# A macaron block of MoE, attention and MoE on one core: an eviction moved to ScalarE and GpSimd, attention's weights loaded among the experts, attention's tiles begun three slots later

## The chip, the core and the metric

The kernel runs on one core of a Trainium2 chip. The core has TensorE (PE: matmuls, with weight loads shown as PEld), VectorE (DVE), ScalarE (ACT), GpSimd (POOL) and SyncE (SP, which here only issues DMAs). Each engine works through its own queue in order and waits on semaphores for the others. The metric is the device time of one execution in microseconds, as a median over runs. A profile is one further execution, recorded instruction by instruction.

## The reference

4096 tokens of 256 channels (2 x 2048) go through three residual steps, with 16 attention heads in groups of 64 tokens, and 8 experts of which each token takes 2:

```python
def ffn(x):                                   # router_w, rg, ru, rd: experts; sg, su, sd: shared
    xn = x * rsqrt(mean(x * x) + eps)
    p, i = top_k(softmax(xn @ router_w.T), 2)
    rw = p / sum(p)
    # each expert takes its first 640 tokens, in token order
    routed = scatter_add(w * ((silu(xg @ rg) * (xg @ ru)) @ rd))      # 256 -> 1024 -> 256
    return (silu(x @ sg) * (x @ su)) @ sd + routed                    # 256 -> 2048 -> 256

def attn(x):
    q, k, v = split(x @ w_qkv)
    q, k = rmsnorm(q) * ln_w, rmsnorm(k) * ln_w
    return (softmax(causal(q @ k.T / 4)) @ v) @ w_proj                # inside groups of 64 tokens

x = x + 0.5 * ffn(layernorm(x))
x = x + attn(layernorm(x))
x = x + 0.5 * ffn(layernorm(x))
```

## The kernel before

Every float32 operand of a matmul is split into a high and a low float16 part, and each product is three matmuls (high x high, high x low, low x high: TERMS, line 35). `split` (line 101) makes such a pair of a weight: ACT scales and casts the high part, DVE subtracts to get the low part.

The shared FFN works on 8 blocks of 512 tokens. `shared` (line 379) runs 16 chunks of 128 hidden columns. In each, `gate_up` (line 326) does 12 matmuls into two PSUM tiles `pgu` (three buffers), ACT applies Silu (or Tanh, with an extra DVE step at line 344), DVE multiplies (line 349), ACT casts to `hh` (line 351) and DVE subtracts to `hl` (line 352). The 12 `down` matmuls of a chunk (line 360) are deferred until after the next chunk's `gate_up`; they add up in two PSUM tiles `outs` of 256 tokens each. After the last chunk, `fin` evicts both: DVE scales a tile and adds the residual `xr` (line 393), and SP stores it (line 396). `late` is the chunk at which the residual is loaded: 2, except for the last block in stage d, where it is 10. The eviction of a block thus stands, in program order, behind the first chunk of the next block.

The routed experts (`experts`, line 422) run one after the other, each with 8 chunks. A chunk loads three float32 pieces by SP (`re`, `re2`, two buffers), splits them on ACT and DVE, and runs 24 + 15 matmuls. After an expert's last chunk its five output tiles `eo` are scaled by the token weights (three on DVE, line 458, two on ACT, line 456), and POOL scatters each with an adding indirect DMA (line 459). There are four `eo` buffers. The five scatters of an expert are declared independent of each other; the first of the next expert waits for them. `expert_load` (line 403) fetches the next expert's tokens and tags.

Attention works on 32 tiles of 128 tokens. `attn_tile` (line 506) is a generator of some 27 steps: load, statistics, normalised `z` (ACT, line 159), transposes by SP, q/k/v (PE), the split into QK (ACT, POOL), scores, softmax (POOL lines 583 and 594, ACT lines 591 and 593), V copies (ACT, line 587), the weighted sum, projection, and statistics and split of the result for the second FFN. The fourth tile of each block then runs `route`, whose last steps are 8 indirect scatters on POOL for that block (line 317).

Four stages follow each other:

- a: the first FFN's front (statistics, routing) for 32 tiles, interleaved with shared blocks 0 to 3.
- b: the 8 experts of the first FFN.
- c: `attn_init` loads and splits attention's weights; then the shared blocks 4 to 7 of the first FFN and blocks 0 to 6 of the second run, 11 blocks and 176 chunks, with the attention tiles interleaved.
- d: the 8 experts of the second FFN, and its shared block 7.

The interleaving is written out: `drive` (line 720) takes one step of the block at a time, and after every three (`RATE_C`, one chunk) makes a slot of `Tiles.steps` (line 685), in which each living tile does one step. A new tile starts at every fourth slot (`GAP_C`), when `slot == nxt * gap`. At the end of a block, the whole last slot is emitted at once. That fixes the program order; the order on each engine is then made by the framework, which schedules by a simulated timeline (line 857) and may bring work forward whose inputs and buffers are free. SP's queue carries all loads, stores and transposes; POOL's carries the indirect DMAs beside its arithmetic.

Lines the change touches: `fin` in `shared` (388 to 398), `experts` (422, 453, 462, 467), `attn_init` (471 to 486), and the start of stage c in `macaron` (806 to 812).

Of the kernel before, what the change touches and what calls it, by code (L numbers as in the profile page):

```python
# [8 lines left out]
F32 = mybir.dt.float32  # L9
F32R = mybir.dt.float32r  # L10
F16 = mybir.dt.float16
# [4 lines left out]
ALU = mybir.AluOpType  # L16
# [4 lines left out]
P = 128  # L21
H = 256
# [3 lines left out]
WS = 16.0  # L26
XP = UP * WS
NB = 8
BT = 512
# [8 lines left out]
class Net:  # L38
# [340 lines left out]
    def shared(self, b, xb, src, dst, tanh=False, late=2):  # L379
        nc = self.nc  # L380
        outs = [self.ps_out.tile([P, BT], F32, name="po", tag="po") for _ in range(2)]
        for c in range(16):
            if c == late:
                res = self.res_load(src, b)
            h = [a[:, 0:BT] for a in self.hbuf()]
            yield from self.gate_up(self.sgu[:, c], xb, h, tanh)

            def fin(c=c, h=h):
                self.down(outs, 4, h, self.sdw[:, :, c], c, 16)
                if c < 15:  # L390
                    return
                for i in range(2):
                    nc.vector.scalar_tensor_tensor(
                        out=res[i], in0=outs[i].rearrange("p (t f) -> p t f", f=H), scalar=0.5 / WS,
                        in1=res[i], op0=ALU.mult, op1=ALU.add)
# [23 lines left out]
            out=w, in0=tag[:, :, 3], scalar=float(e), in1=tag[:, :, 1], op0=ALU.is_equal, op1=ALU.mult)  # L419
        nc.vector.tensor_tensor(out=w, in0=w, in1=tag[:, :, 2], op=ALU.add)  # L420

    def experts(self, R, rg, ru, rd, cur):

        nc = self.nc
        for e in range(E):
            x, ids, wts = cur["x"], cur["id"], cur["w"]
            outs = [self.ps_out.tile([P, BT], F32, name="po", tag="po") for _ in range(3)]
            cur = {}
            nxt = self.expert_load(R, e + 1, cur) if e < E - 1 else iter(())
            for c in range(8):  # L430
                r = self.raw.tile([P, 2, 2, P], F32, name="re", tag="raw")
                for i, s in enumerate((rg, ru)):
                    nc.sync.dma_start(
                        out=r[:, i], in_=s[e, :, c * P:(c + 1) * P].rearrange("(k p) f -> p k f", p=P))
                r2 = self.raw.tile([P, H], F32, name="re2", tag="raw2")
                nc.sync.dma_start(out=r2, in_=rd[e, c * P:(c + 1) * P])
                wc = self.raw.tile([P, 2, 2, 2, P], F16, name="wc")
                self.split(wc[:, 0], wc[:, 1], r)
                wd = self.raw.tile([P, 2, H], F16, name="wd")
                self.split(wd[:, 0], wd[:, 1], r2)  # L440
                h = self.hbuf()
                for t0, n in SUBS:
                    hs = [a[:, t0:t0 + n] for a in h]
                    for _ in self.gate_up(wc, x[:, :, t0:t0 + n], hs):
                        pass

                def fin(e=e, c=c, h=h, wd=wd, outs=outs, ids=ids, wts=wts):
                    self.down(outs, 5, h, wd, c, 8)
                    if c < 7:
                        return  # L450
                    key = R["key"], e
                    for t in range(5):
                        eo = self.raw.tile([P, H], F32, name="eo", bufs=4)
                        o = outs[t // 2][:, (t % 2) * H:(t % 2 + 1) * H]
                        if t % 2:
                            nc.scalar.activation(eo, o, AF.Copy, scale=wts[:, t:t + 1])
                        else:
                            nc.vector.tensor_scalar_mul(eo, o, wts[:, t:t + 1])  # L458
                        i = nc.gpsimd.indirect_dma_start(  # L459
                            out=R["acc"][:, :], out_offset=bass.IndirectOffsetOnAxis(ap=ids[:, t:t + 1], axis=0),  # L460
                            in_=eo, in_offset=None, bounds_check=T - 1, oob_is_err=False, compute_op=ALU.add).ins
                        if t:
                            self.tc.declare_no_dep(i, group=str(key), reason="an expert's tokens are distinct")
                        self.tc.add_to_no_dep_group(str(key), i)

                self.defer(fin)
                next(nxt, None)
            for _ in nxt:
                pass

    def attn_init(self, w_qkv, ln_w, w_proj):
        nc = self.nc
        a = self.at
        self.wqkv = a.tile([P, 2, 2, 3 * H], F16, name="wqkv")
        self.wpr = a.tile([P, 2, 2, H], F16, name="wpr")
        for k in range(2):
            for c0, n in ((0, 2 * H), (2 * H, H)):
                r = a.tile([P, 2 * H], F32, name="rq", tag="q32")[:, :n]
                nc.sync.dma_start(out=r, in_=w_qkv[k * P:(k + 1) * P, c0:c0 + n])
                self.split(self.wqkv[:, 0, k, c0:c0 + n], self.wqkv[:, 1, k, c0:c0 + n], r)  # L480
        wp = w_proj.rearrange("(j r c) f -> r j c f", r=2, c=16)
        for k in range(2):
            r = a.tile([P, H], F32, name="rp", tag="yy")
            for j in range(8):
                nc.sync.dma_start(out=r[j * 16:(j + 1) * 16], in_=wp[k, j])
            self.split(self.wpr[:, 0, k], self.wpr[:, 1, k], r)
# [227 lines left out]
def run_slots(tiles, until):  # L714
    while not until():
        for _ in tiles.steps():
            pass
# [22 lines left out]
def macaron(ctx, tc, x, w_qkv, ln_w, w_proj, router_w, rg, ru, rd, sg, su, sd, out):  # L740
    nc = tc.nc
    x = x.rearrange("b s h -> (b s) h")
    out = out.rearrange("b s h -> (b s) h")
    n = Net(ctx, tc)
    R1 = n.route_init(0)
# [5 lines left out]
    first = {}, {}  # L751
# [36 lines left out]
    def all_shared(key, b, src, dst, **k):  # L788
        yield from n.shared(b, fbs[key]["xb"], src, dst, **k)
        used.add(key)  # L790

    with n.phase("a", BT, 2, 16):
# [5 lines left out]
        tiles = Tiles(tile1, 32, GAP_A)  # L798
# [5 lines left out]
            drive(fed(main, weights) if b == 0 else main, tiles, RATE_A)  # L804
        run_slots(tiles, tiles.done)
    with n.phase("b", CAP, 3):
        n.experts(R1, rg, ru, rd, first[0])
    with n.phase("c", BT, 2, 6, SLC):
        n.attn_init(w_qkv, ln_w, w_proj)
        tiles = Tiles(tile2, 32, GAP_C)  # L810
        for b in range(NA, NB):
            drive(all_shared((1, b), b, R1["acc"], R1["acc"], tanh=True), tiles, RATE_C)
        for b in range(NC):
            run_slots(tiles, ready(2, b))
            drive(all_shared((2, b), b, x2, R2["acc"], tanh=True), tiles, RATE_C)
        run_slots(tiles, tiles.done)
# [16 lines left out]
SLC = 2  # L833
# [28 lines left out]
```

## Time and profile before

| what | us |
|---|---|
| median of 3 runs | 1830.85 (1830.73 to 1833.56) |
| the profiled execution's own time | 1834.82 |
| its span, first to last instruction | 1833.1 |
| PE busy in it | 1779.5 (97%) |
| DVE, ACT, POOL busy | 1199.9, 952.9, 751.3 |
| mean granted TensorE clock | 0.998 of full speed |

In time order, stage b is full from about 295 to 605, stage c begins at 605 and its last evictions are at 1453, and stage d takes the rest.

A timeline row reads: start, duration, engine, line, operation, output<-inputs, shape, count; in square brackets, how long the engine had stood idle before it and what ended that. A group row has its count after the x, then busy time and the mean in nanoseconds, then the idle time before the group with what ended it. A stretch row gives the stretch, its length, and the busy time of PE, PEld, DVE, ACT and POOL (instructions after the x), the granted clock, the share of DMA engines busy and GB/s. Idle time of an engine costs something only where PE waits for it in the end.

### The profile page before, as it was taken

Reading aid. Unit: us, or ns where it says so; the run is one execution under the profiler, and the core shown is the slowest. Engines: PE = TensorE matmul, PEld = TensorE weight load, DVE = VectorE, ACT = ScalarE, POOL = GpSimd, SP = SyncE. Lnnn points to the kernel's source line nnn. Section 1 sums busy time; section 2 is a strip of 40 time slices with the busy share of each in tenths; the row PEclk is TensorE's granted clock in tenths of the full one; section 3 lists DMA queues with packets and bytes.
Section 4 is the critical chain, followed back from the end, with each engine's and each line's share of the span. In section 5 each row is a group of like instructions: output and inputs, shape, how many; then the busy total and the mean of one; then the engine's idle time right before and its main releaser. Section 6 shows DMA issues by size and latency. Waiting matters only on the chain.

```text
span 1833.1 us, 37526 instructions
## 1 busy us (share of the span) xinstructions
PE 1779.5 (97%) x13724; PEld 1197.0 (65%) x13724; DVE 1199.9 (65%) x2891; ACT 952.9 (52%) x2055; POOL 751.3 (41%) x1072
## 2 busy tenths in 40 slices
PE   7899999999999899999999999999999999999998
PEld 4555556777777556666666666665655677777765
DVE  7754445666666567878777878787656566666643
ACT  5433234555555366666666666666323455555542
POOL 6755530112211334567767676776430011112210
PEclk9999999999999999999999999999999999999999
DMA  7532042455543346668576776766213044455420
GB/s 219 146 90 77 3 88 54 107 118 124 118 113 90 73 77 112 122 118 146 113 146 124 133 142 117 144 101 126 52 27 80 28 111 111 107 120 122 102 47 12
DMA packets 439194, 185.96 MB, mean 101 GB/s; under 512 B 302305, under 2 KB 436125, under 8 KB 439008
## 3 DMA queue, kind: packets, MB, share of 16 engines
q1 hardware_dynamic: 420528, 161.60, 40.7%
q0 software_dynamic: 17664, 21.17, 6.5%
q8 instruction: 107, 1.75, 0.4%
q10 hardware_dynamic: 816, 0.79, 0.1%
q14 instruction: 79, 0.65, 0.1%
HBM read 78.95 MB, written 42.21 MB: 66 GB/s over the span
## 4 chain that ended last, share of the span: by engine, by line
PE 36%; issue 32%; POOL 12%; DVE 10%; DMA 5%; ACT 4%; SPq 0%; POOLq 0%; another core or an unknown queue 0%; DVEq 0%; ACTq 0%
PE pgu L336 22%; PE po L360 11%; POOL xg L317 3%; DVE sl L349 2%; DMA acc<-eo,eidscatter 2%; DVE sl L344 1%; DVE hl L352 1%; POOL X L315 1%; POOL rstd L149 1%; POOL acc L459 1%; ACT hh L351 1%; PE pqk L636 1%; POOL S L583 1%; DVE st L144 1%; POOL e L594 1%
## 5 line engine op out<-in xcount | busy, mean ns | idle before, releaser
L336 PE MATMUL pgu<-xb,sgu 128*128 128x512 f16 x3072 | 742.4, 380 | 18.1 <-DVE sl L349 7.7
L351 ACT CAST hh<-sl 128x512 f16<-128x512 f32 (+2 forms) x512 | 272.8, 533 | 482.9 <-DVE sl L349 466.6
L336 PE MATMUL pgu<-xe,wc 128*128 128x384 f16 (+1 forms) x3072 | 497.0, 299 | 0.0
L336 PEld LDWEIGHTS <-sgu 128*128 128x128 f16 x3072 | 293.4, 98 | 292.9 <-issue 25.8
L349 DVE SCALAR_TENSOR_TENSOR sl<-pgu,sl 128x512 f32<-128x512 f32 (+2 forms) x512 | 300.2, 587 | 227.3 <-PE pgu L336 193.4
L352 DVE TENSOR_TENSOR hl<-sl,hh 128x512 f16<-128x512 f32 (+2 forms) x512 | 311.2, 608 | 161.5 <-ACT hh L351 155.1
L360 PEld LDWEIGHTS <-hh 128*128 128x128 f16 x3328 | 320.3, 98 | 112.3 <-ACT hh L351 7.9
L336 PEld LDWEIGHTS <-wc 128*128 128x128 f16 x3072 | 300.5, 98 | 92.0
L360 PE MATMUL po<-sdw,hh 128*128 128x256 f16 x2048 | 350.1, 273 | 8.1 <-issue 2.8
L360 PE MATMUL po<-sdw,hl 128*128 128x256 f16 x1024 | 247.1, 273 | 14.3 <-DVE hl L352 13.4
L360 PE MATMUL po<-wd,hh 128*128 128x256 f16 x1280 | 223.6, 273 | 0.0
L459 POOL DMA_INDIRECT out_dram<-eo,eidscatter x40 | 65.1, 1627 | 342.1 <-DVE eo L458 332.3
L360 PEld LDWEIGHTS <-hl 128*128 128x128 f16 x1664 | 162.8, 98 | 58.6 <-DVE hl L352 24.2
L347 ACT ACTIVATE sl<-pgu 128x384 f32<-128x384 f32 (+1 forms) x336 | 158.9, 473 | 71.1 <-PE pgu L336 35.5
L459 POOL DMA_INDIRECT acc<-eo,eidscatter x40 | 65.7, 1643 | 296.5 <-DVE eo L458 286.8
L317 POOL DMA_INDIRECT xg<-X,di x128 | 132.3, 1034 | 70.4 <-issue 27.5
L360 PE MATMUL po<-wd,hl 128*128 128x256 f16 x640 | 152.5, 273 | 1.1 <-DVE hl L352 1.1
L344 DVE SCALAR_TENSOR_TENSOR sl<-sl,pgu 128x512 f32<-128x512 f32 x176 | 119.9, 681 | 48.1 <-ACT sl L343 46.1
L343 ACT ACTIVATE sl<-pgu 128x512 f32<-128x512 f32 x176 | 104.2, 593 | 45.3 <-PE pgu L336 39.7
L104 ACT ACTIVATE wc<-re 128x512 f16<-128x512 f32 x128 | 80.5, 629 | 67.9 <-PE pgu L336 57.6
L105 DVE SCALAR_TENSOR_TENSOR wc<-re,wc 128x512 f16<-128x512 f32 x128 | 88.3, 690 | 22.9 <-ACT wc L104 22.6
L583 POOL TENSOR_TENSOR S<-S,amx 128x1024 f32<-128x1024 f32 x32 | 62.0, 1938 | 79.0 <-DVE amx L582 72.1
(150 smaller groups left out, 1713.3 us busy)
## 6 DMA issues: line engine op xcount, KB each, us to landing
re<-in_L_ffn_rg_dram SPq DMA_DIRECT2D x128, 128.0 KB
re<-in_L_ffn_ru_dram SPq DMA_DIRECT2D x128, 128.0 KB
re<-in_L_ffn_rd_dram SPq DMA_DIRECT2D x128, 128.0 KB
y<-acc SPq DMA_DIRECT2D x64, 128.0 KB
y<-in_L_attn_x_dram SPq DMA_DIRECT2D x32, 128.0 KB
acc<-xr SPq DMA_DIRECT2D x16, 256.0 KB
out_dram<-xr SPq DMA_DIRECT2D x16, 256.0 KB
x<-y SPq DMA_DIRECT2D x28, 128.0 KB
```

What stands on the lines that cost most here:

```text
L104: nc.scalar.mul(hi, src, WS)
L105: nc.vector.scalar_tensor_tensor(out=lo, in0=src, scalar=WS, in1=hi, op0=ALU.mult, op1=ALU.subtract)
L317: i = nc.gpsimd.indirect_dma_start(out=R["xg"][:, :], out_offset=bass.IndirectOffsetOnAxis(ap=di[:, t, k:k + 1], axis=0), in_=X, in_offset ...
L336: nc.tensor.matmul(p, lhsT=wc[:, w, i, k, :], rhs=x[:, 2 * a + k, :], start=(j == 0), stop=(j == 5))
L343: nc.scalar.activation(s, p, AF.Tanh, scale=0.5 / XP)
L344: nc.vector.scalar_tensor_tensor(out=s, in0=s, scalar=1.0, in1=p, op0=ALU.add, op1=ALU.mult)
L347: self.latest[0] = nc.scalar.activation(s, p, AF.Silu, scale=1.0 / XP).ins
L349: self.latest[1] = nc.vector.scalar_tensor_tensor(out=s, in0=ps[1], scalar=1.0 / XP / (2.0 * XP if tanh else 1.0), in1=s, op0=ALU.mult, op ...
L351: nc.scalar.copy(h[0], s)
L352: nc.vector.tensor_tensor(out=h[1], in0=s, in1=h[0], op=ALU.subtract)
L360: nc.tensor.matmul(o, lhsT=h[a][:, t * P:(t + 1) * P], rhs=wd[:, w], start=(c == 0 and j == 0 and t % 2 == 0), stop=(c == nch - 1 and j == 2),
L459: i = nc.gpsimd.indirect_dma_start(out=R["acc"][:, :], out_offset=bass.IndirectOffsetOnAxis(ap=ids[:, t:t + 1], axis=0), in_=eo, in_offset ...
```

## The change

In the blocks whose residual is loaded early (15 of 16) the second tile is scaled by ACT into a buffer `ev`, and POOL adds the residual; the first stays on DVE. The experts have five `eo` buffers, and the fifth scatter of an expert is no longer declared independent of the four before it. Attention's weights are loaded and split in stage b, by a generator that `experts` advances after chunks 3 and 6 of each expert (16 times), in eight pieces of 256 columns through one buffer; they now lie in the constant pool. In stage c ten buffers `X` replace six, and the slot counter starts at -3, so that the first tile begins after three chunks.

```diff
@@ shared, fin @@
                 for i in range(2):
-                    nc.vector.scalar_tensor_tensor(
-                        out=res[i], in0=outs[i].rearrange("p (t f) -> p t f", f=H), scalar=0.5 / WS,
-                        in1=res[i], op0=ALU.mult, op1=ALU.add)
+                    o = outs[i].rearrange("p (t f) -> p t f", f=H)
+                    if i == 0 or late > 2:
+                        nc.vector.scalar_tensor_tensor(
+                            out=res[i], in0=o, scalar=0.5 / WS, in1=res[i], op0=ALU.mult, op1=ALU.add)
+                    else:
+                        ev = self.tok.tile([P, 2, H], F32, name="ev", bufs=1)
+                        nc.scalar.mul(ev, o, 0.5 / WS)
+                        nc.gpsimd.tensor_tensor(out=res[i], in0=ev, in1=res[i], op=ALU.add)
                     nc.sync.dma_start(
...
-    def experts(self, R, rg, ru, rd, cur):
+    def experts(self, R, rg, ru, rd, cur, also=iter(())):
...
-                        eo = self.raw.tile([P, H], F32, name="eo", bufs=4)
+                        eo = self.raw.tile([P, H], F32, name="eo", bufs=5)
...
-                        if t:
+                        if 0 < t < 4:
                             self.tc.declare_no_dep(i, group=str(key), reason="an expert's tokens are distinct")
...
                 next(nxt, None)
+                if c in (3, 6):
+                    next(also, None)
...
-    def attn_init(self, w_qkv, ln_w, w_proj):
-        self.wqkv = a.tile([P, 2, 2, 3 * H], F16, name="wqkv")
-        self.wpr = a.tile([P, 2, 2, H], F16, name="wpr")
-        for k in range(2):
-            for c0, n in ((0, 2 * H), (2 * H, H)):
-                r = a.tile([P, 2 * H], F32, name="rq", tag="q32")[:, :n]
-                nc.sync.dma_start(out=r, in_=w_qkv[k * P:(k + 1) * P, c0:c0 + n])
-                self.split(self.wqkv[:, 0, k, c0:c0 + n], self.wqkv[:, 1, k, c0:c0 + n], r)
+    def attn_weights(self, w_qkv, w_proj):
+        nc = self.nc
+        self.wqkv = self.cst.tile([P, 2, 2, 3 * H], F16, name="wqkv")
+        self.wpr = self.cst.tile([P, 2, 2, H], F16, name="wpr")
         wp = w_proj.rearrange("(j r c) f -> r j c f", r=2, c=16)
         for k in range(2):
-            r = a.tile([P, H], F32, name="rp", tag="yy")
+            for c0 in (0, H, 2 * H):
+                r = self.raw.tile([P, H], F32, name="rq", bufs=1)
+                nc.sync.dma_start(out=r, in_=w_qkv[k * P:(k + 1) * P, c0:c0 + H])
+                yield
+                self.split(self.wqkv[:, 0, k, c0:c0 + H], self.wqkv[:, 1, k, c0:c0 + H], r)
+                yield
+            r = self.raw.tile([P, H], F32, name="rq", bufs=1)
             for j in range(8):
                 nc.sync.dma_start(out=r[j * 16:(j + 1) * 16], in_=wp[k, j])
+            yield
             self.split(self.wpr[:, 0, k], self.wpr[:, 1, k], r)
+            yield
+
+    def attn_init(self, ln_w):
...
     with n.phase("b", CAP, 3):
-        n.experts(R1, rg, ru, rd, first[0])
-    with n.phase("c", BT, 2, 6, SLC):
-        n.attn_init(w_qkv, ln_w, w_proj)
+        n.experts(R1, rg, ru, rd, first[0], n.attn_weights(w_qkv, w_proj))
+    with n.phase("c", BT, 2, 10, SLC):
+        n.attn_init(ln_w)
         tiles = Tiles(tile2, 32, GAP_C)
+        tiles.slot = -3
```

More of the change, by code (lines that the diff above doesn't have):

```diff
@@ L467, in experts @@
                 next(nxt, None)
+                if c in (3, 6):
+                    next(also, None)
             for _ in nxt:
                 pass
[L471 removed]
+    def attn_weights(self, w_qkv, w_proj):
+        nc = self.nc
+        self.wqkv = self.cst.tile([P, 2, 2, 3 * H], F16, name="wqkv")
+        self.wpr = self.cst.tile([P, 2, 2, H], F16, name="wpr")
+        wp = w_proj.rearrange("(j r c) f -> r j c f", r=2, c=16)
+        for k in range(2):
+            for c0 in (0, H, 2 * H):
[5 more added lines that the diff above has]
+            r = self.raw.tile([P, H], F32, name="rq", bufs=1)
+            for j in range(8):
+                nc.sync.dma_start(out=r[j * 16:(j + 1) * 16], in_=wp[k, j])
+            yield
+            self.split(self.wpr[:, 0, k], self.wpr[:, 1, k], r)
+            yield
+    def attn_init(self, ln_w):
         nc = self.nc
         a = self.at
[L474 to L486 removed]
         self.lnw = a.tile([P, H], F32, name="lnw")
```

## The prediction

> **What bounds the kernel.** I read the page's busy shares first, then PE's busy time in 20 us stretches, then PE's timeline at every gap, then the other engines' timelines there.
>
> ```profile
> PE 1779.5 (97%) x13724; PEld 1197.0 (65%) x13724; DVE 1199.9 (65%) x2891; ACT 952.9 (52%) x2055; POOL 751.3 (41%) x1072
> ```
>
> TensorE has work for 1779.5 of 1833.1 us, and the change alters no matmul. So only the 53.6 us in which PE is idle can move. The stretches place them: 20.9 us before 140, 2.0 in 140-240, 4.0 in 240-300 (experts of the first FFN start), 0.3 in 300-600, 6.7 in 600-680 (attention starts), 9.7 in 840-1260, 1.0 in 1260-1360, 3.3 in 1360-1400, 0.8 at 1498, 4.9 at the end.
>
> Around 611-637, from the timelines of PE, DVE and ACT:
>
> ```profile
> 611.35 1.46 PE L336 MATMUL pgu<-xb,sgu 128*128 128x512 f16 x6 [0.39 <-DVE sl L344]
> 614.25 2.75 PE L336 MATMUL pgu<-xb,sgu 128*128 128x512 f16 x12 [1.45 <-DVE sl L349]
> ...
> 624.59 0.61 PE L360 MATMUL po<-sdw,hh 128*128 128x256 f16 x4 [0.45 <-ACT hh L351]
> ...
> 628.33 0.61 PE L360 MATMUL po<-sdw,hh 128*128 128x256 f16 x4 [1.10 <-ACT hh L351]
> ```
>
> ```profile
> 613.11 0.48 DVE L458 TENSOR_SCALAR eo<-po,ewscatter 128x256 f32<-128x256 f32 x1 [1.82 <-DMA acc<-eo,eidscatter]
> ```
>
> ```profile
> 623.40 0.63 ACT L104 ACTIVATE wqkv<-rq 128x512 f16<-128x512 f32 x1 [4.04 <-DMA rq<-in_L_attn_w_qkv_dram]
> ```
>
> The number in brackets is idle time, with what ended it. DVE stands 1.82 us at its fifth eo, since four buffers are still being scattered, and PE then starves behind DVE (0.39 + 1.45). ACT next stands behind weight pieces that haven't landed, and the casts hh queued after them come late.
>
> In attention's steady stage PE is full, save at block ends:
>
> ```profile
> 846.25 1.46 PE L336 MATMUL pgu<-xb,sgu 128*128 128x512 f16 x6 [0.87 <-DVE sl L344]
> ...
> 849.44 0.28 PE L360 MATMUL po<-sdw,hl 128*128 128x256 f16 x1 [0.71 <-DVE hl L352]
> ```
>
> The pair comes back at 927, 1008, 1089, 1169 and 1250: 6 x 1.58 = 9.5 us. It is absent at the block ends of 689 and 767, before the first routing. The routing's scatters fill POOL just ahead of it (stretches: PE, PEld, DVE, ACT, POOL busy):
>
> ```profile
> 820.00:840.00 20.00, 20.00 (x181) 12.93 (x179) 14.67 (x36) 12.19 (x23) 18.53 (x30) 1.00 0.67 144
> 840.00:860.00 20.00, 18.42 (x150) 11.14 (x149) 16.35 (x41) 13.45 (x30) 11.60 (x16) 1.00 0.81 161
> ```
>
> POOL's late rstd holds the z of two tiles, ACT's backlog holds the tanh of the new block (844.89), hence 0.87. Then DVE runs evict, mask add, evict before hl: hence 0.71.
>
> **The change, part by part** (us; minus is gain).
>
> *Five eo buffers.* The fifth evict no longer waits for the first scatter. Gone with it: 0.39 + 1.45 at 611-614, 0.28 at 340.34 and 0.77 at 1498.72, the first expert of each set: **-2.9**. DVE waits there at all 16 experts (13.7 + 16.3 us), but PE shows no gap at the rest, so those are worth nothing.
>
> *The fifth scatter now waits for its expert's four before it.* Those land about 3.9 us after issue (616.68 + 3.92), so the last lands near 622.7 instead of 620.6: 618.75, when the fourth issued at 614.83 lands, plus 3.9. Behind it on POOL stand only attention's memsets and, 29 us later, the next expert's scatters. SP's y<-acc and xr<-acc wait for it, but they went at 626.11 and 626.58 before. Tile 0 now begins after chunk 3, near 621, and xr is needed only at 689. **0**, and up to +2 were the cover gone.
>
> *Attention's weights leave the start of attention.* Six splits with their in-order waits go from ACT and DVE, 20 loads from SP. The gaps after 624 go: 0.45 + 1.10 + 0.27 + 0.23 + 0.85 = **-2.9**.
>
> *They appear among the experts*: 22 loads, 8 splits at 0.40 on ACT and 0.42 on DVE, so 3.2 and 3.4 us over a stage where ACT has 10.8 and DVE 12.4 busy of each 20 us and PE is full. The work is hidden; where it lands isn't sure. The order is made by a simulated timeline that moves ready work far ahead: the tags of all seven later experts are read at 266-280, up to 270 us ahead of their experts. The weight chain (one buffer, load, split, load) can be pulled there too, into loads that are late already:
>
> ```profile
> 264.09 0.63 ACT L104 ACTIVATE wc<-re 128x512 f16<-128x512 f32 x1 [2.74 <-DMA re<-in_L_ffn_ru_dram]
> ```
>
> PE loses 4.0 us there now. Bounds 0 (each piece waits out its five chunks) and +4 (as much again). Nearest row: the same weights cost 2.9 at attention's start. I take half: **+1.5**. The eight 16-partition proj loads take SP some 4.1 us a time (628.38), behind which expert loads queue; two chunks of buffers cover that.
>
> *First tiles.* At 660.86 (1.19) and 666.95 (0.41) PE waits while tiles 0 and 1, bunched by the late weights, collide. Three slots later, with weights present, tile 0 starts clean. Bounds 0 and -1.6; I take **-0.8**. The delay itself costs nothing: tiles fill 128 of 176 slots, their last matmuls end near 1320, the stage's last evictions are at 1453; 3 slots are 12-15 us.
>
> *The evictions*, 15 of 16 blocks. The row removed and the nearest rows to those added:
>
> ```profile
> L393 DVE SCALAR_TENSOR_TENSOR xr<-po,xr 128x512 f32<-128x512 f32 x32 | 21.3, 682 | 6.2 <-PE po L360 6.1
> ...
> L343 ACT ACTIVATE sl<-pgu 128x512 f32<-128x512 f32 x176 | 104.2, 593 | 45.3 <-PE pgu L336 39.7 <-remote 2.7 <-PE po L360 0.5
> ...
> L583 POOL TENSOR_TENSOR S<-S,amx 128x1024 f32<-128x1024 f32 x32 | 62.0, 1938 | 79.0 <-DVE amx L582 72.1 <-DVE rc L608 6.9
> ```
>
> DVE loses 0.68 a block (0.60 of pace), ACT gains 0.59, POOL about 1938/2 = 0.97. A rule speaks against this. Row first:
>
> ```profile
> 693.82 2.13 POOL L594 TENSOR_TENSOR e<-S,e 128x1024 f16<-128x1024 f32 x1 [4.63 <-ACT e L593]
> ...
> 694.29 2.20 DVE L352 TENSOR_TENSOR hl<-sl,hh 128x512 f16<-128x512 f32 x1 [1.33 <-ACT hh L351]
> ```
>
> hl takes 0.69 elsewhere; here it ends 0.54 after POOL's instruction. The Trainium skill (SBUF — State Buffer, "Who interferes with whom") says that a DVE instruction with two SBUF inputs is blocked outright by a GpSimd instruction that reads SBUF, one input not at all. The old evict has one input in PSUM and blocks nobody; the new add has two in SBUF and can hold the very hl that PE waits for. By plain rows a block end gains 0.60, over six 3.6, and the sum below would be -9.7; by the rule, if the two collide each time, it loses 0.97 - 0.60 = 0.37, over six 2.2, and the sum would be -3.9. No row shows where the add will fall, so half and half: (-0.60 + 0.37)/2 = -0.12, x 6 = -0.7.
>
> *The shift against blocks.* Tile work that fell at a block end now falls three chunks into the next; the block end meets what came at 832. Splitting 1.58 apart: the 0.87 is routing's echo and goes along; the 0.71 needs two evicts beside mask add, and should shrink. I take another -0.25 x 6 = -1.5, so **-2.2** for block ends. Bounds: -9.5 (all go) and +10 (next part). SP's store of xr waits for the add, with QT transposes and y loads behind it; in 820-840 PE stayed full with POOL at 18.5, so a few us of that are covered. Ten X buffers: no wait on X's scatter shows after 620, **0**. The 3.3 at 1360-1400 (DVE waiting on the second experts' tags) comes 12-15 us later and may meet the block end of 1394 or miss it: bounds -3.3 and +2, I take **0**.
>
> *First FFN, four block ends.* SP's store at 95.42 waits for POOL, which is busy to 98, and the y load at 96.44, on the chain of waits, stands behind it. Bounds -0.5 and +3; I take **+0.5**.
>
> Sum: -2.9 - 2.9 + 1.5 - 0.8 - 2.2 + 0.5 = **-6.8**. From the profiled execution: 1834.82 (span 1833.1 and 1.7 around it) gives 1828.0. The median of the runs shown is 4.0 lower than that execution; the gaps are the same program's, so 1830.85 - 6.8 = **1824.1**.
>
> **Rivals.** (a) *The alignment dissolves the block-end gaps*: -7.3 in place of -2.2 with the rest kept, -11.9 to -14 with the tail's 3.3 partly gone: 1817-1819. For: both gaps need routing, tile phase and evicts together. Against: 0.87 stems from POOL's saturation alone. (b) *Gains cancelled*: the weights' waits reappear whole at 260-300 (+3 to +4) and block ends stay (0): -2.9 - 2.9 + 3.5 - 0.8 + 0.5 = -2.6: 1828.3. (c) *Slower*: the scatter stretch (old 816-841, POOL full) moves onto the block end. The add queues in it, lengthens it by 0.97 a block, and holds hl and the z behind it; all of a block's last slot is emitted in one go there. Price per block end against today: x on seven. Without block ends the sum is -4.6, so it loses from x = 0.7, and by more than 0.2% from x = 1.2, about the add plus a blocked hl. At x = 1.5: +5.9, 1836.8. Against: PE rode out the full POOL at 820-840.
>
> **How the numbers follow.** Forecast 0.45, (a) 0.18, (b) 0.17, (c) 0.20. Within 0.2% (3.7 us), about what a measurement of this kernel can tell from no change, lies (b). Faster 0.63, same 0.17, slower 0.20. The forecast's own range is 1820-1827; with the lower end of (a) and (c) up to x = 1.4 (1836), it is 1817 to 1836, which leaves out about 0.06 below and 0.12 above.
>
> **What would show it.** No DVE eo waiting on a scatter and no gap at 611-614, 340 and 1498; attention's start full; ACT waits on rq, if any, with PE gaps at 260-300; per block end, hl no longer than 0.7 and a gap under 1.3. Wrong: hl of 1.2-1.7 beside the add, gaps over 2 us at block ends, or POOL full for 30 us on end.

## The result

The changed kernel takes 1848.39 us (median of 6 runs, 1846.66 to 1849.82), the kernel before 1832.25 on the same chip (1830.73 to 1837.23). The ratio is 1.008, 95% interval 1.0069 to 1.0091: **slower by 13 to 17 us**, where I had forecast 6.8 us faster and a range that ended at 1836.

The profiled execution of the changed kernel takes 1849.82 us, its span is 1848.1, which is 15.0 longer than before. Busy shares, from its page:

```profile
PE 1783.1 (96%) x13724; PEld 1199.3 (65%) x13724; DVE 1216.2 (66%) x2878; ACT 964.1 (52%) x2072; POOL 780.8 (42%) x1087
```

PE's idle time grew from 53.6 to 65.0 us (+11.4), and the same matmuls kept it busy 3.6 us longer. The gaps in PE's timeline, summed by stretch (those of 0.15 us and more, 48.0 before and 58.7 after):

| stretch, us | what runs | before | after |
|---|---|---|---|
| 0-140 | first FFN | 20.7 | 19.3 |
| 240-300 | experts start | 4.1 | 6.7 |
| 600-680 | attention starts | 6.3 | 6.0 |
| 840-1290 | attention, steady | 10.1 | 18.6 |
| 1360-1430 | attention ends | 3.2 | 3.3 |
| 1430-1490 | second experts start | 0.0 | 2.6 |

**Block ends.** PE's timeline of the changed kernel at the first block end after routing has begun:

```profile
847.47 0.28 PE L360 MATMUL po<-sdw,hl 128*128 128x256 f16 x1 [0.58 <-DVE hl L352]
...
851.47 0.28 PE L360 MATMUL po<-sdw,hl 128*128 128x256 f16 x1 [1.76 <-DVE hl L352]
...
858.65 0.39 PE L588 MATMUL psc<-QT 128*128 128x64 f16 x8 [0.59 <-DVE qk L558]
```

Three gaps of 2.93 us in all stand where a pair of 1.58 stood, six times over; the third, 14 us behind the evictions, waits for attention's qk. The timeline of DVE and POOL beside them:

```profile
844.81 2.60 DVE L352 TENSOR_TENSOR hl<-sl,hh 128x512 f16<-128x512 f32 x1
844.94 1.92 POOL L597 TENSOR_TENSOR S<-S,amx 128x1024 f32<-128x1024 f32 x1
...
849.33 2.08 DVE L352 TENSOR_TENSOR hl<-sl,hh 128x512 f16<-128x512 f32 x1
849.58 1.28 POOL L400 TENSOR_TENSOR xr<-ev,xr 128x512 f32<-128x512 f32 x1
```

An hl that has DVE to itself takes 0.69. Here two of them last 2.60 and 2.08, and each ends 0.55 us after a POOL instruction with two SBUF inputs: the softmax's S<-S and the new add. Summed over attention's steady stage (840 to 1290, the excess over 0.69 of every hl that took over 1.0), DVE lost 4.3 us on 11 such instructions before, and 24.4 us on 22 after.

**Attention's start.** The same view around 620 to 631, all engines:

```profile
620.27 1.55 POOL L464 DMA_INDIRECT acc<-eo,eidscatter  x1 [2.98 <-DVE sl L344]
...
624.12 0.89 SPq L374 DMA_DIRECT2D xr<-acc  x2
624.46 2.66 POOL L512 MEMSET QK<- 128x3072 f16 x1 [2.47 <-PE pgu L336]
...
627.44 0.20 DVE L510 COPY mask<-m 64x64 f32<-64x64 f32 x1 [7.41 <-POOL mask L507]
628.77 0.82 DVE L144 BATCH_NORM_STATS2 st<-y 128x6 f32<-128x256 f32 x2 [1.13 <-DMA y<-acc]
...
629.59 0.66 DVE L349 SCALAR_TENSOR_TENSOR sl<-pgu,sl 128x512 f32<-128x512 f32 x1
...
630.29 2.72 PE L336 MATMUL pgu<-xb,sgu 128*128 128x512 f16 x6 [5.17 <-DVE sl L349]
```

The gaps of the weights are gone, and one of 5.17 has come: POOL's memsets wait for the fifth scatter, DVE's mask copy for POOL, and the sl that PE needs stands behind the copy and behind the statistics of a y that was loaded late. (The memset's row names PE. By the trace's semaphores POOL's queue had stood before it until the fifth scatter landed at 624.10; SP's load of acc, which waits for that scatter too, goes at 624.12.) The six matmuls after the gap took 2.72 us, where six took 1.46 before; the view by stretches has busy us (and instructions) of PE, PEld, DVE, ACT and POOL, and then the granted clock, 0.83:

```profile
620.00:640.00 20.00, 14.83 (x79) 8.23 (x78) 9.57 (x32) 6.56 (x13) 9.48 (x15) 0.83 0.39 108
```

**The second experts' start.** The timelines of ACT and PE:

```profile
1465.28 0.60 ACT L399 ACTIVATE ev<-po 128x512 f32<-128x512 f32 x1 [3.94 <-PE po L360]
1465.90 1.28 ACT L347 ACT_TABLE_LOAD   x1
1467.19 0.76 ACT L347 ACTIVATE sl<-pgu 128x384 f32<-128x384 f32 x2
...
1467.73 4.26 PE L336 MATMUL pgu<-xe,wc 128*128 128x256 f16 x18 [2.55 <-ACT sl L347]
```

The eviction, now on ACT, waits 3.94 us for the block's last matmul; the table load for the expert's Silu and the Silu itself stand behind it, and PE is idle for 2.55.

### The profile page after: what moved, and what is told of

It reads as the page before. It is cut to its first block, busy times and chain, and to the rows that moved or that the text cites. A ratio compares the mean times of both kernels' runs of the same rounds, so it can differ in the third digit from the quotient of the medians.

```text
span 1848.1 us, 37550 instructions
## 1 busy us (share of the span) xinstructions
PE 1783.1 (96%) x13724; PEld 1199.3 (65%) x13724; DVE 1216.2 (66%) x2878; ACT 964.1 (52%) x2072; POOL 780.8 (42%) x1087
## 3 DMA queue, kind: packets, MB, share of 16 engines
q8 instruction: 107, 1.75, 0.4%
## 4 chain that ended last, share of the span: by engine, by line
PE 42%; POOL 8%; DVE 6%; issue 3%; DMA 3%; ACT 2%; SPq 0%; POOLq 0%; DVEq 0%; ACTq 0%
PE pgu L336 26%; PE po L360 13%; POOL xg L317 3%; DMA QT<-QK 1%; DVE sl L349 1%; DVE sl L344 1%; PE pqk L650 1%; POOL X L315 1%; PE py L619 1%; POOL xa L169 1%; DMA y<-acc 1%; DVE hl L352 1%; POOL rstd L149 1%; DMA yt<-yp 1%; DVE amx L596 1%
## 5 line engine op out<-in xcount | busy, mean ns | idle before, releaser
L336 PE MATMUL pgu<-xb,sgu 128*128 128x512 f16 x3072 | 743.1, 381 | 13.4 <-DVE sl L349 6.6
L352 DVE TENSOR_TENSOR hl<-sl,hh 128x512 f16<-128x512 f32 (+2 forms) x512 | 335.0, 654 | 169.9 <-ACT hh L351 156.9
L360 PE MATMUL po<-sdw,hl 128*128 128x256 f16 x1024 | 248.7, 274 | 21.2 <-DVE hl L352 19.2
L360 PE MATMUL po<-wd,hl 128*128 128x256 f16 x640 | 148.4, 273 | 0.0
```

The lines of the kernel that those rows point to most:

```text
L336: nc.tensor.matmul(p, lhsT=wc[:, w, i, k, :], rhs=x[:, 2 * a + k, :], start=(j == 0), stop=(j == 5))
L352: nc.vector.tensor_tensor(out=h[1], in0=s, in1=h[0], op=ALU.subtract)
L360: nc.tensor.matmul(o, lhsT=h[a][:, t * P:(t + 1) * P], rhs=wd[:, w], start=(c == 0 and j == 0 and t % 2 == 0), stop=(c == nch - 1 and j == 2),
```

## The experiments

My first theory was that eviction and delay share the blame at the block ends; the rivals were the eviction alone and the delay alone. The first four kernels each undo one part of the change. A part's worth is read as a difference of ratios, times 1832 us. Where a part is undone, the intervals of two ratios enter, and the worth is known to about 3 us either way (an estimate from these intervals).

**Both evictions on DVE again** (the rest of the change kept).

```
-                    if i == 0 or late > 2:
+                    if True:
```

> The changed kernel with both evictions on DVE again, everything else kept. My theory (the evictions and the shift share the blame at the block ends: the add falls into the full POOL stretch that the shift moved there): the 1.76 at each block end drops to about 0.7, the pairs of 0.58 and 0.59 stay, because S<-S,amx still holds hl; 6 x 1.05 = 6.3 back. The 2.55 at 1467 and the 1.13 at 296, both behind an eviction on ACT, go too: 3.7. Together -10 against the changed kernel, a ratio to the kernel before of about 1.0035. Rival 1 (the evictions alone are to blame): the whole 1.35 x 6 and the 3.7, so -12 and a ratio of 1.002 or less. Rival 2 (the shift alone is to blame): only the 3.7 comes back, ratio 1.007.

Measured: 1.0110 (1.0095 to 1.0126), slower still by 5.5 us than the whole change. My theory and both rivals had expected a gain. The add is gone, and of the gaps behind hl only 0.34 a block is left (8.7 us lost by hl in place of 24.4), but the block ends keep 2.7 to 3.6 in another form (0.84 to 1.40, 1.51, 0.34 at most of them), now mainly behind ACT's hh. So moving the eviction helps here, but not by fewer waits: in the profiled execution, the fastest of the four, PE is idle for 62.0 us, 3.0 less than in the changed kernel, and its matmuls take 3.5 longer (1786.6), at a mean granted clock of 0.994 (0.993 to 0.995 in all four executions, against 0.995 to 0.998 in the changed kernel's six). Why the clock is lower is open.

**Tiles at slot 0.**

```
-        tiles.slot = -3
```

> The changed kernel with attention's tiles beginning at slot 0 again, everything else kept. My theory (shared blame): the full POOL stretch lies some 12 us ahead of the block end again, the three gaps of 2.93 fall back to 1.6 or less (-8), the tail's 3.3 lies at 1360-1400 as before (0), the two first tiles collide again (+1): -7, a ratio of about 1.005. Rival 1 (evictions alone): the block ends keep their 2.9, ratio 1.0085. Rival 2 (shift alone): -8 and the slow clock with it, ratio 1.003.

Measured: 1.0006 (0.9997 to 1.0014). Rival 2 holds and is exceeded: without the delay the change costs nothing that can be measured, so the delay costs 13.6 us here. (The ten X buffers stayed, so they are not the cause.) Each block end shows a single gap of 0.88; the second of the old pair, 0.71, is gone with the eviction.

**Four eo buffers, fifth scatter free.**

```
-                        eo = self.raw.tile([P, H], F32, name="eo", bufs=5)
+                        eo = self.raw.tile([P, H], F32, name="eo", bufs=4)
...
-                        if 0 < t < 4:
+                        if t:
```

> The changed kernel with four eo buffers, and with the fifth scatter free of its four predecessors, as before; everything else kept. My theory (the waiting fifth scatter keeps POOL's memsets, and behind them DVE's mask copy, until 627.4, and PE then stands 5.17 us with a lowered clock after it): the copy comes at about 624, the gap shrinks to about 2 and the clock stays up: -4.4; the gaps at 611-614, 340 and 1498 return: +2.9. Net -1.5, ratio about 1.0075, and no gap over 2.5 at 625-632. Rival (the mask is late anyway, behind POOL's memsets): the gap stays, +2.9, ratio 1.0095.

Measured: 1.0075 (1.0061 to 1.0089), as expected by my theory, though the interval takes in no difference from the change. The 5.17 shrank to 0.75 and 0.76, the clock stayed up, and 1.47 at 617 and 0.79 at 343 came back. But the mask copy still came at 627.68, after 4.49 us of idle DVE: the mask was no earlier, PE was later, by the gaps that had come back. What the gap at attention's start hangs on was still open.

**Attention's weights at its start again.** The two calls and the two functions as they were before, the rest kept.

> The changed kernel with attention's weights loaded and split at attention's start again, none among the experts; everything else kept. My theory: the 7.1 us of idle at 240-300 fall back to 4.0 (-3.1); at attention's start the weights' waits run beside the wait for the mask, which is as long, so nothing is added there or about +1: -2 to -3, ratio about 1.007. Rival (the weights among the experts are hidden, and the 3 us at 260-300 have another cause, such as POOL or the order of the expert loads): 240-300 keeps about 7 us of idle, and attention's start grows by 2.9, ratio 1.0095.

Measured: 1.0064 (1.0050 to 1.0077). Idle time in 240-300 falls from 6.7 to 4.3; attention's start has 6.6 instead of 6.0. That is what my theory says, and 2.9 us by the ratios; but the two intervals overlap, and all of PE's idle time in the two profiles is about the same (65.7 here, 65.0 in the change), so this kernel alone does not show it.

The next kernels take the delay alone, another delay, and two suspected causes at slot 0.

**The delay alone**, added to the kernel before.

```
-    with n.phase("c", BT, 2, 6, SLC):
+    with n.phase("c", BT, 2, 10, SLC):
...
         tiles = Tiles(tile2, 32, GAP_C)
+        tiles.slot = -3
```

> The kernel before with one thing added: attention's tiles begin three slots later (and ten X buffers). My theory now (the shift is the cause: it lays routing's full POOL stretch onto the block end): with both evictions on DVE the block ends go from 1.58 to about 2.8 each, as in the run with the evictions undone (2.7 to 2.9): +7.5; the tail's wait comes about 15 us later and meets a block end, +1; first tiles -1; ratio 1.004 to 1.005. Rival (the shift does harm only together with the new scatter wait or the moved weights): block ends stay at 1.6 or less, ratio 1.000.

Measured: 1.0073 (1.0059 to 1.0087). The delay by itself costs 13.4 us, more than I expected even then. Its block end, all engines:

```profile
845.07 0.97 POOL L317 DMA_INDIRECT xg<-X,di  x1 [0.30 <-issue]
...
846.06 1.92 POOL L583 TENSOR_TENSOR S<-S,amx 128x1024 f32<-128x1024 f32 x1
...
848.01 1.06 ACT L591 ACTIVATE S<-S 128x1024 f32<-128x1024 f32 x1 [5.01 <-POOL S L583]
848.97 0.60 ACT L351 CAST hh<-sl 128x512 f16<-128x512 f32 x1
...
849.63 0.61 PE L360 MATMUL po<-sdw,hh 128*128 128x256 f16 x4 [0.90 <-ACT hh L351]
```

At this block end no hl is held (over the stage hl loses 8.7 us, 4.1 of it in one block). S<-S waits on POOL behind four scatters in a row (840.79 to 846.04), ACT waits 5.01 us in order for S, and hh comes behind it. Over the stage ACT's Exp waits 26.9 us for S, six times, against 12.9 before; in the changed kernel, where ACT has an eviction more, it is 5.1, and hl is held instead. Two routes, the same loss: 18.5 and 18.6 us of gaps. The span of this profile is 12.8 longer than before: 8.4 of it lie in these gaps, and 3.7 in matmuls that take longer, the granted clock being 0.91 and 0.92 in the two stretches of 1400-1440.

**Eight slots of delay** (the change with `tiles.slot = -8`).

> The changed kernel with eight slots of delay in place of three; everything else kept. A slot is one chunk of 4.9 us and a block is 16, so the full POOL stretch, which begins 29 us ahead of the block end at slot 0 and lies on it at three, would begin 10 us behind it at eight. My theory (it is the phase that counts): block ends fall to 0.9 each or less, 12 us below the changed kernel; the tail, 39 us later than before, is unsure by 3. Ratio about 1.002. Rival (a later attention costs by itself, since its tiles run closer to the end of the blocks that need them): block ends stay near 2.9, ratio 1.008 or more.

Measured: 1.0022 (1.0014 to 1.0030). From ACT's and PE's timelines:

```profile
917.35 0.59 ACT L399 ACTIVATE ev<-po 128x512 f32<-128x512 f32 x1
...
956.80 0.39 PE L588 MATMUL psc<-QT 128*128 128x64 f16 x8 [1.35 <-DVE vs L553]
...
998.71 0.59 ACT L399 ACTIVATE ev<-po 128x512 f32<-128x512 f32 x1
...
1018.73 1.46 PE L336 MATMUL pgu<-xb,sgu 128*128 128x512 f16 x6 [0.64 <-DVE sl L344]
```

The block ends themselves (the ev rows) are free of gaps, as my theory expected. What it did not expect are two gaps per block further on, of 0.64 and 1.36, 20 and 39 us behind the evictions; hl loses 7.3 us, and 840-1290 has 11.3 us of gaps in place of 18.6. So later is not worse by itself: it is the phase. It isn't as good as slot 0.

**The mask built early**, at slot 0. The lines of `attn_init` that make it move to a function called ahead of `experts`; the mask lies in `cst`.

> The changed kernel with slot 0, and with the causal mask (two memsets, two selects, one copy) built in the first stage's constants instead of at attention's start. My theory (DVE's mask copy stands behind POOL's QK memset, which waits for the last scatter): against the same kernel with the late mask (ratio 1.0006) the gaps of 3.23 and 1.03 at 627 to 631 and the lowered clock there go: -4 to -5, ratio about 0.998. Rival (BN stats wait for the same scatter through y<-acc, and hold sl as long without the mask): the gap stays above 2.5, ratio 1.000 or more.

Measured: 1.0022 (1.0013 to 1.0032), not faster, and the gap stays. The rival's row:

```profile
621.89 1.55 POOL L464 DMA_INDIRECT acc<-eo,eidscatter  x1 [2.84 <-issue]
...
627.67 0.43 DVE L144 BATCH_NORM_STATS2 st<-y 128x6 f32<-128x256 f32 x1 [7.21 <-DMA y<-acc]
...
628.74 2.33 PE L336 MATMUL pgu<-xb,sgu 128*128 128x512 f16 x6 [3.16 <-DVE sl L344]
```

DVE stands 7.21 us at tile 0's statistics, whose y is loaded after the last scatter has landed. My theory of the mask falls: whatever DVE has next in order that needs the scatter holds it. (Why this kernel is 3 us slower than the one with the late mask, I can't say; its block ends are the same, and PE's idle time in its profile is no longer, 53.8 against 54.7.)

**Both evictions on DVE in the two blocks ahead of the experts**, at slot 0.

```
-                    if i == 0 or late > 2:
+                    if i == 0 or late > 2 or (b == NA - 1 and not tanh) or (b == NC - 1 and src is not dst):
```

> The changed kernel with slot 0, and with both evictions on DVE in the two blocks after which the experts begin (the last of the first FFN's four, and the last of attention's stage). My theory (ACT's eviction waits in order for PE's last po, and the expert's first Silu with its table load stands behind it): the 2.55 at 1456 and the 1.13 at 297 go, and the clock there stays up: -3.7, ratio about 0.9986. Rival (the Silu is late by itself, through the table load or the expert's weights): both gaps stay, ratio 1.0006.

Measured: 0.9991 (0.9983 to 0.9998). The 2.55 and the 1.13 are gone; 1.76 has come at 297. The theory holds: 2.7 us against slot 0 alone, 3.7 expected.

The next kernels add parts to the kernel before.

**The evictions alone.**

> The kernel before with one thing added: one of a block's two evictions on ACT with the add on POOL, as in the change. My theory (DVE, eased by one eviction, no longer delays hl at the block end; ACT's eviction delays the expert's first Silu): the 0.71 at six block ends goes (-4.3), the 0.87 stays, a gap of about 2.5 appears before the second experts and one of about 1 before the first (+3.6): ratio 0.9995. Rival (the add's two SBUF inputs hold DVE's hl, or wait in POOL's queue, at the block end): block ends stay at 1.58 or more, ratio 1.002.

Measured: 0.9995 (0.9987 to 1.0004), as expected. At its block ends:

```profile
844.15 1.46 PE L336 MATMUL pgu<-xb,sgu 128*128 128x512 f16 x6 [0.87 <-DVE sl L344]
...
846.00 0.68 DVE L352 TENSOR_TENSOR hl<-sl,hh 128x512 f16<-128x512 f32 x1
...
846.12 1.70 POOL L400 TENSOR_TENSOR xr<-ev,xr 128x512 f32<-128x512 f32 x1 [0.85 <-ACT ev L399]
```

The 0.87 stays, the 0.71 is gone at every one. The add comes to an idle POOL while hl runs: hl takes its 0.68, and the add 1.70 in place of 1.28, at all six. The gap of 2.55 stands at 1449.63.

**The evictions alone, but not ahead of the experts** (the two edits above together, on the kernel before).

> The kernel before with the moved eviction in all blocks but the two after which experts begin (those keep both on DVE). My theory: -4.3 at the block ends and no gap before the experts: ratio 0.9977. Rival as for the run with all the evictions: 1.000.

Measured: **0.9966 (0.9952 to 0.9980), 1824.96 us against 1831.45**, the fastest of all, better than both kernels. Its table load no longer waits for the block's last matmul, which ends at 1443.30; ACT:

```profile
1438.84 0.62 ACT L351 CAST hh<-sl 128x512 f16<-128x512 f32 x1 [2.24 <-DVE sl L349]
1440.26 1.28 ACT L347 ACT_TABLE_LOAD   x1 [0.80 <-DVE hl L352]
```

**Five eo buffers with the waiting fifth scatter alone.**

> The kernel before with one thing added: five eo buffers, the fifth scatter waiting for its expert's four. My theory (the gaps at 611 to 614, 340 and 1498 go, -2.9; the last scatter lands near 624, about 3 later, and y's load after it, but ACT and DVE stand there for the weights anyway): ratio 0.9985 to 0.9995. Rival (the late scatter costs at attention's start what the buffers gain, as in the changed kernel): a gap of 2 or more at 625 to 632, ratio 1.000 to 1.001.

Measured: 1.0018 (1.0011 to 1.0026). The rival holds:

```profile
614.61 1.55 POOL L459 DMA_INDIRECT acc<-eo,eidscatter  x1 [3.02 <-DVE sl L344]
...
621.28 0.63 ACT L104 ACTIVATE wqkv<-rq 128x512 f16<-128x512 f32 x1 [7.67 <-DMA rq<-in_L_attn_w_qkv_dram]
...
623.63 1.91 PE L336 MATMUL pgu<-xb,sgu 128*128 128x512 f16 x6 [4.21 <-DVE sl L349]
```

The 1.45 at 614 is gone, and 4.21 has come at 623: ACT's wait for the first weight piece grew from 4.04 to 7.67. The weights were no cover; they came later with the scatter. Their first load is another instruction that waits for it: by the trace's semaphores SP sends it at 618.45, when the fifth scatter has landed at 618.37, and before at 620.69, when it had landed at 620.60. Five buffers without the wait were not run, so what they are worth by themselves is known from the gaps alone.

**Tile 0's statistics two chunks later**, with the early mask, slot 0, and DVE evictions ahead of the experts.

```
+        if j == 0:
+            yield
+            yield
         mv = self.sm.tile([P, 2], F32, name="amv")
         rstd = self.sm.tile([P, 1], F32, name="arstd")
-        self.stats(y, mv, rstd)
+        with self.behind(j == 0, 1):
+            self.stats(y, mv, rstd)
```

> The changed kernel with slot 0, the two evictions ahead of the experts on DVE, the mask built early, and tile 0's BN stats put two chunks later, behind DVE's sl of that time. My theory (with the mask away, DVE stands at tile 0's BN stats, which wait for a y whose load waits for the late fifth scatter, and sl is queued behind them): the gaps of 3.14 and 1.12 at 625 to 628 and the clock of 0.83 there go: -5 against the same kernel without the two moves (0.9991), ratio 0.9965. Rival (something else that waits for the scatter holds PE there, such as the slow clock's own cause): a gap over 2 stays at 624 to 640, ratio 0.999.

Measured: 0.9992 (0.9984 to 1.0001), no gain over 0.9991. The gaps at 625-628 and the lowered clock there are gone, as the theory says of the cause; but 2.69 us come back at 643.57 behind ACT, which then waits 2.83 for tile 0's transposed input (the 1.76 at 297 stays too, now 1.75 at 302). The wait was moved, not removed.

The last four kernels ask what the delay brings onto the block end, the scatters or the tiles, and what the weights are worth alone.

**The delay, with the scatters four slots later again.** Four more yields ahead of the scatter loop of the second routing (and ten X buffers).

```
+        if R["key"] == "scatter1":
+            for _ in range(4):
+                yield
         for t in range(4):
```

> The kernel before with tiles three slots later (as in the run of the shift alone, 1.0073), and the routing's scatters of attention's stage four slots later again, so that they lie behind the block end. Theory A (the scatters on the block end do the harm: S<-S,amx waits behind them on POOL, ACT's Exp waits in order for S, and the casts hh stand behind the Exp): the three gaps per block end (0.9 + 1.5 + 0.3) shrink to 1.6 or less in all, ratio 1.001 or less. Theory B (the tiles' own work does it): they stay near 2.8, ratio 1.007.

Measured: 1.0036 (1.0022 to 1.0050), between the two. The block ends are clear, and the gap has followed the scatters 20 us on:

```profile
864.39 3.08 DVE L355 TENSOR_TENSOR hl<-sl,hh 128x512 f16<-128x512 f32 x1 [1.98 <-ACT e L596]
...
864.76 2.15 POOL L597 TENSOR_TENSOR e<-S,e 128x1024 f16<-128x1024 f32 x1
...
867.52 0.28 PE L363 MATMUL po<-sdw,hl 128*128 128x256 f16 x1 [2.26 <-DVE ve L147]
```

(lines shifted by three; PE's row names a short DVE instruction that ends with hl, at 867.5). hl loses 22.1 us in this kernel, Exp waits 18.2.

**Only the scatters four slots later**, tiles at slot 0 (the same yields and the ten X buffers without the delay).

> The kernel before with tiles at slot 0, and only the routing's scatters of attention's stage four slots later (20 us), onto the block end. Theory A (scatters): block ends grow from 1.58 to about 2.8, ratio 1.004 or more. Theory B (tiles): they stay at 1.6 or fall, since POOL is free ahead of the block end; ratio 1.000 or less.

Measured: 1.0009 (1.0002 to 1.0017). The gaps per block are 2.5 (1.07 and 1.41, both behind hl, which loses 16.6 us), near theory A; the total is not, since other stretches of this kernel lost less (240-300: 2.3; 600-680: 4.5). So neither theory holds alone. Moving the scatters moves the gaps and changes what collides; the block end is not needed for them.

**The weights alone**, on the kernel before.

> The kernel before with one thing added: attention's weights loaded and split among the first experts. Theory: 240-300 grows from 4.0 to about 6.5 us of idle, attention's start falls from 6.3 to about 3 (DVE still stands for tile 0's y, but the last scatter is not late here): net -1, ratio 0.9995. Rival (the pieces are hidden among the experts): 240-300 stays at 4, ratio 0.998. Rival (the start's gaps come back behind y, as in the changed kernel): 600-680 stays at 6, ratio 1.001.

Measured: 1.0015 (1.0007 to 1.0022). Idle 5.6 in 240-300, 2.4 in 300-600 where there was 0.3, and 5.5 at attention's start where there was 6.3. The second rival: the start keeps its gaps, behind y. What the pieces hold among the experts, from ACT, DVE and PE:

```profile
302.12 0.42 ACT L104 ACTIVATE wpr<-rq 128x256 f16<-128x256 f32 x1 [3.47 <-DMA rq<-in_L_attn_w_proj_dram]
...
302.57 0.43 DVE L105 SCALAR_TENSOR_TENSOR wpr<-rq,wpr 128x256 f16<-128x256 f32 x1 [2.32 <-ACT wpr L104]
302.91 0.42 DVE L349 SCALAR_TENSOR_TENSOR sl<-pgu,sl 128x256 f32<-128x256 f32 x1
...
303.38 0.82 PE L336 MATMUL pgu<-xe,wc 128*128 128x256 f16 x6 [1.88 <-DVE sl L349]
```

ACT stands for the last piece, DVE for ACT, and the sl that PE needs stands behind both, as the hh did at attention's start. The 1.76 at 297 and the 1.75 at 302 above are this same wait.

**The best kernel with the weights among the experts.**

> The kernel before with the moved eviction in all blocks but the two ahead of the experts (0.9966), and with attention's weights among the experts as well. If the weights are worth -1: ratio 0.996. If they are hidden: 0.995. If attention's start keeps its gaps: 0.998.

Measured: 0.9981 (0.9974 to 0.9988): 2.7 us worse than without, about what the two intervals can tell apart, and the same 2.7 as alone. No gain is left in that part.

## Why the prediction was wrong

The four parts, each alone on the kernel before and each undone from the change, in us of 1832:

| part | forecast | alone (95%) | in the change |
|---|---|---|---|
| three slots of delay | -1.5 - 0.8 | +13.4 (10.8 to 15.9) | +13.6 |
| five eo buffers and the waiting scatter | -2.9 + 0 | +3.3 (2.0 to 4.8) | +0.9 |
| weights among the experts | -2.9 + 1.5 | +2.7 (1.3 to 4.0) | +2.9 |
| evictions | -0.7 + 0.5 | -0.9 (-2.4 to +0.7) | -5.5 |
| sum | -6.8 | +18.5 | +11.9 |

The change itself is at +14.7 by its ratio (12.6 to 16.7), between the two sums. In the last column only the delay, and more narrowly the evictions, stand clear of the 3 us either way.

*The shift against blocks: this step failed, and it is most of the error.* I wrote that the 0.87 goes along with routing's echo and the 0.71 should shrink, and took -1.5; of the delay itself I wrote that it costs nothing. It costs 13.4. What I left out is that the phase sets which of DVE's and POOL's two-input instructions run side by side and where S<-S stands in POOL's queue. Rival (c) had named the place and the mechanism, the POOL stretch on the block end with the add queued in it and hl held, and was given 0.20. Its size at the block ends was near, 1.35 against the 1.5 that I worked with. But it blamed the add as well, and the run of the delay alone loses as much with no add in it. Which work on POOL does the harm, the scatters or the tiles' own, stays open: moving either moves the gaps. The evidence that I set against it, PE full at 820-840 beside a full POOL, was evidence for that phase only.

*The fifth scatter waits: "0, and up to +2 were the cover gone" failed.* The landing near 622.7 was 1.4 us early: the scatter was issued at 620.27 and landed at 624.10. The list of what stands behind it was the error. It held POOL's memsets and SP's loads, and stopped there: behind the memsets stands DVE's mask copy, behind y's load DVE's statistics, and behind both, in order, the sl that PE waits for. That is what the late scatter held in each of the kernels above.

*Five buffers: right.* The 1.45 at 614, the 0.28 at 340 and the 0.77 at 1498 went, 2.5 of the 2.9; the 0.39 at 611 stayed. It was outweighed by the wait that comes with it.

*The weights leave the start: right in the row, wrong in the sum.* The five gaps that I listed after 624 went. But alone the change of start is worth 0.8 and not 2.9, since y's wait takes the place of the weights'.

*The weights appear among the experts: the place was right, the term too small.* The chain of pieces is pulled forward to 266-298 in the changed kernel, as feared. Where I took +1.5, the weights alone lose 1.6 in 240-300 and 2.1 in 300-600, inside the bounds of 0 and 4. (The step from 4.1 to 6.7 in the profile of the change holds 1.13 of the eviction.) I had thought of expert loads that come later; the largest gap, 1.88, is ACT and DVE standing in order for the piece itself.

*First tiles:* 1.60 became 0.42, the forecast's -0.8 was -1.2. *Tail:* forecast 0; 3.2 became 3.3, now on the block end of 1403 with a clock of 0.83 in its 20 us.

*The evictions: the total was right by luck, the parts were not.* By plain rows the gap of 0.71 should go, and at slot 0 it went at every block end (-4.3 over six, where I took half of 0.60). Not in the sum at all was that an eviction on ACT waits in order for the last matmul of its block and so holds the first Silu of the stage after it: 2.55 and 1.13. I looked behind the add on POOL and not behind the eviction on ACT. The +0.5 for the first FFN can't be read: its idle time is 21.5 with the evictions alone and 19.2 with the best kernel, which share nearly all of that stage. The add itself takes 1.28; half of a 1024-element row had given 0.97.

The rule weighed there (the Trainium skill, SBUF — State Buffer, "Who interferes with whom") is borne out by the rows: a two-input hl and a two-input POOL instruction exclude each other, and, as the same section says, it is not the instructions but their order that decides who waits. At slot 0 the add, which comes to an idle POOL, waits 0.42 for hl; three slots later, where it follows a scatter without a pause, hl ends 1.39 us late. (The recorded start of hl is the earlier one in both, by 0.12 and 0.25, so the record alone doesn't tell who will be held.) My price by the rule, 0.37 net a block end, was too low for the second case and not due in the first, and half and half of the two was neither.

The rest of the loss is PE's clock: its matmuls take 3.6 us longer of the 15.0 in the profiled execution, and the clock is lowered where the new waits stand (0.83 in 620-640, 0.83 in 1400-1420, 0.91 in 1460-1480; before 0.91 in 100-120 alone, the last 20 us aside).

## What to carry to other kernels

A step that only moves work in time is not free: before pricing it at its own length, list which instructions of two engines it newly sets side by side, and what stands in the slowest queue ahead of the value that the bound engine needs. Behind a wait that is added, follow every queue to the end, through the engines that wait for the ones that wait, and do the same for an instruction moved to another engine: what was harmless at the end of DVE's queue held the next stage's first instruction on ACT. And when a stall disappears, ask what else waits for the same event; here the weights, the mask and y all stood on the last scatter, and taking one away showed the next.

## What the hardware showed

- hl (DVE, two SBUF inputs) that met a POOL two-input instruction ended 0.55 us after it, whether that took 1.28 or 1.92. Where two POOL instructions followed each other, hl stayed out through both: 3.08 us for one of 0.69, across yp (864.13) and e (864.76 to 866.91). POOL's side pays when it is second: 1.70 for 1.28.
- The granted clock fell to 0.83 or 0.91 over a 20 us stretch after each PE gap of 3.1 to 5.2 us at attention's start (3.14, 3.16, 3.23, 4.21, 5.01, 5.16, 5.17). After the same gap of 2.55 at the second experts' start it fell in two kernels of seven. The Trainium skill (TensorE: Matmul & The Clock Gate, Part 1) puts the fall after an idle window of about 3.4 us that runs free of the kernel; gaps somewhat shorter than that are enough at times here.
- Kernels with the same block ends can differ by 2 to 3 us elsewhere: the gaps of 240-300 come to 2.3, 3.4, 3.9 and 4.1 us in four kernels whose edits all lie behind that stretch. A part's worth to 1 us can't be read from one kernel alone.
